# Self-attention's last two units and the context factors of batch 1: packed reciprocals, a GpSimd block, three borrowed tiles

## The chip, the cores and the metric

The kernel runs on one core of a Trainium2 chip. Its time is the device time of one execution in microseconds (us). The core has a matrix engine (TensorE, "PE" in the profile, its weight loads "PEld"), a vector engine (VectorE, "DVE"), an activation engine (ScalarE, "ACT"), a general engine (GpSimd, "POOL") and a sync engine (SyncE, "SP") that here issues nearly all DMAs. Each engine runs its instructions in order; semaphores tie them together.

## The reference, cut to what matters

```
x = x + xcond(layernorm(x), cond, ctx)      # x: 2 x 1024 tokens x 256, fp32
x = x + ffn(layernorm(x))

xcond(x):  h = adaln(x);  x = x + softmax(q k^T / 8) v @ wo + bo   # self-attention, 16 heads of 64
           h = adaln(x);  x = x + cross-attention(h, ctx) @ wo + bo # 16 heads, 77 context rows
           h = adaln(x);  x = x + (a * gelu(gate)) @ w2 + b2        # a, gate = split(h @ w1 + b1)
ffn(x):    two "bit-linear" layers (activations rounded to 8 bits, weights to -1, 0, 1), gelu between
```

## The kernel before, in words

**Self-attention** is cut into 32 units u = 0 to 31 (batch, pair of heads, half of the queries), each with 8 blocks kb of 128 keys. A tile of a block is 128 keys x 1024 (two heads x 512 queries). The order of the work of PE, DVE, ACT and POOL is written by hand in a loop over slots, two blocks to a slot and four slots (q = 0 to 3) to a unit; SP's DMAs are placed by the tile framework's scheduler. In slot s:

- PE makes the scores of two blocks into one of two double PSUM banks (pool ps2, tag "s"), ACT copies them out to sT (L941), DVE takes the running maximum macc (L363).
- After a unit's last block, the maximum over keys is folded: DVE transposes (max_turned, L368), reduces (max_folded, L372 to L385), SP writes the row of 1024 maxima to DRAM (md, L386) and reads it back broadcast to 128 partitions (wide, L387). Two slots later max_placed copies wide into PSUM (mb, ACT L391).
- DVE subtracts mb from a block (shifted, L400); block 5 (POOL_KB) is subtracted on POOL instead (L395), except in unit 31. ACT takes exp (L404), POOL adds the blocks up in pacc (L411), PE multiplies by v (times_v, L419), seven slots after the scores.
- The row sums: PE multiplies pacc by ones. For units 0 to 29 the sums come out packed in four quarters (L451), go through DRAM to a small tile "few" (sums_packed), DVE inverts 128 x 8 numbers (inverted_packed, L482), and they come back broadcast as rinv. For units 30 and 31 the sums come out broadcast (sums_by_ones, L440; unit 31 sums sT itself block by block into tot_last), and DVE inverts 4 x 128 columns in place (inverted, L492). POOL multiplies the unit's output aT by rinv (normalised, L495).

**Cross-attention** has been turned into two small factors per batch, G (scores = h1T x G, 128 x 2464 numbers) and U (output = p x U), kept in DRAM as gd and ud. Its 16 blocks of 128 tokens, each in two halves of 8 heads, run as: cross_scores (PE, L748, bank "s"), cross_shifted (DVE maximum L763 and subtraction L766), cross_exp (ACT L775), cross_divided (DVE L780, L781; POOL L782), cross_turned (PE transposes pt_a and pt_b, L794; ACT and DVE copies pT, L802 to L805), cross_out (PE L815), cross_added (DVE L827). Blocks 0 to 2 of it (the dictionary "tail") start while the last two units of self-attention finish (slots 128 to 133); po_last (L281) is self-attention's last output product. Blocks 3 to 15 run in a second hand-written loop, whose step n makes scores for block n and output for block n - 1.

G and U live in a pool "gu" with two buffers. The G of batch 1 therefore takes the buffer of batch 0's G when block 7 has made its scores (load_g(1), L722), and the U of batch 1 that of batch 0's U (load_u(1), L728 to L732).

**The ternary weights** of the last layers are made in the same loop: DVE and POOL scale, clip and round raw into wq (bf16), PE transposes them (ternary_turned, pt_w, L1116, in the PSUM bank with tag "f"), ACT copies the result to w1T and w2T (L1118, L1120).

**The feed-forward stage** (pu L1582, po L1608) and the bit-linear layers follow in an order that a small planner writes with assumed costs. It is a second hand-ordered stretch, and the framework's scheduler may set instructions of it among the last of the first.

Of the kernel before, what the change touches and what calls it, by code (L numbers as in the profile page):

```python
# [43 lines left out]
def block_kernel(ctx: ExitStack, tc: tile.TileContext, a: dict, out: bass.AP):  # L44
# [8 lines left out]
    def two_banks(name):  # L53
        return ps2.tile([P, 1024], FP, tag="s", name=name)
# [131 lines left out]
    with ExitStack() as sa:  # L186
# [202 lines left out]
        def max_placed(u):  # L389
            mbs[u] = psx.tile([P, 1024], FP, tag="mb", name="mb")  # L390
            nc.scalar.copy(mbs[u], wides[u])  # L391

            if u < NU - 1:
                t = sT[u, POOL_KB]
                nc.gpsimd.tensor_tensor(t, t, wides[u], ALU.subtract)  # L395

        def shifted(u, kb):
            if kb == POOL_KB and u < NU - 1:
                return
            nc.vector.tensor_tensor(sT[u, kb], sT[u, kb], mbs[u], ALU.subtract)  # L400

# [57 lines left out]
        def summed(u):  # L459

            if u in paccs:
                tots[u] = two_banks("tot")
                if u < NU - 2:
                    sums_in_quarters(tots[u], paccs.pop(u))
                else:
                    sums_by_ones(tots[u], paccs.pop(u), True, True)
            rinvs[u] = p1.tile([P, 512], FP, tag="rinv", name="rinv")
            n = 256 if u < NU - 2 else 512
            nc.scalar.copy(rinvs[u][:, :n], tots.pop(u)[:, :n])

        def sums_packed(u):
# [243 lines left out]

        Gs, Us = {}, {}

        def load_g(b):
            Gs[b] = gu.tile([P, GU], FP, tag="gu", name="G")[:, : DC * HK].rearrange(
                "p (c k) -> p c k", c=DC  # L720
            )
            nc.sync.dma_start(out=Gs[b], in_=gd[b])  # L722

        def load_u(b):
            Us[b] = gu.tile([P, GU], FP, tag="gu", name="U").rearrange("p (c d) -> p c d", d=D)
# [9 lines left out]


        norms, prs2, scs2 = {}, {}, {}
        HB = 4

        def cross_scores(n, half):  # L740

            b, qb = n // TB, n % TB
            hT = norms[1, b].hT
            sc = two_banks("sc2")
            for i in range(2):
                at = (half * 2 + i) * HB * CTX
                for c in range(DC):
                    nc.tensor.matmul(  # L748
                        sc[:, i * 512 : i * 512 + HB * CTX],
                        lhsT=hT[:, c, qb * P : (qb + 1) * P],  # L750
                        rhs=Gs[b][:, c, at : at + HB * CTX],
                        start=(c == 0),
                        stop=(c == DC - 1),
                    )
            scs2[n, half] = sc
# [17 lines left out]
        def cross_exp(n, half):  # L773
            ph = prs2[n, half][:, :HALF]
            nc.scalar.activation(ph, ph, AF.Exp)  # L775
# [156 lines left out]
        def settle():  # L932
            while due:
                due.pop(0)()

        for slot in range(NS + 12):
            u, q = slot // SLOTS, slot % SLOTS

            new = [(u, 2 * q + i, scores(u, 2 * q + i)) for i in range(2)] if slot < NS else []
            for v, kb, sc in new:  # L940
                nc.scalar.copy(sT[v, kb], sc)  # L941
            v, k = (slot - LAG + 1) // SLOTS, (slot - LAG + 1) % SLOTS
            old = [(v, 2 * k + i) for i in range(2)] if 0 <= v < NU else []
            if q:
                settle()
            for job in inner.pop(slot, []):
                job[0](*job[1:])
            if q == 2 and 0 <= u - 1 < NU:
                max_placed(u - 1)
            for at in tail.get(slot, []):  # L950
                cross_scores(*at)

            fold = q == 0 and 0 <= u - 1 < NU
            if q == 2:
                for at in new:
                    running_max(*at)
            late = q == 2 and slot < NS
            if not late:  # L960
                exponentials(old)
            settle()
            if fold:
                max_turned(u - 1)
            if q != 2:
                for at in new:
                    running_max(*at)
            if fold:
                max_folded(u - 1)
            for at in tail.get(slot, []):  # L970
                cross_shifted(*at)
                cross_exp(*at)
            for at in tail.get(slot - 1, []):
                cross_divided(*at)
            if q == 1 and 0 <= u - 3 < NU - 2:
                inverted_packed(u - 3)
            w, k = (slot - LAG) // SLOTS, (slot - LAG) % SLOTS
            if 0 <= w < NU:
                for i in range(2):
                    if w == NU - 1:  # L980
                        if k + i == 0:
                            tots[w] = piece_bank("tot_last")
                        sums_by_ones(tots[w], sT[w, 2 * k + i], k + i == 0, k == SLOTS - 1 and i == 1)
                    times_v(w, 2 * k + i)
                if k == SLOTS - 1:
                    evacuated(w)
            if slot == NS + 6:
                summed(NU - 1)
                for part in range(4):
                    inverted(NU - 1, part)  # L990
                normalised(NU - 1)
            elif q == 2 and 0 <= u - 3 < NU - 2:
                normalised(u - 3)
            elif slot == NS + 5:
                for part in range(4):
                    inverted(NU - 2, part)
                normalised(NU - 2)
            for job in extras.pop(slot, []):
                job[0](*job[1:])
            if slot in (NS + 7, NS + 8):  # L1000
                n = slot - NS - 7
                cross_turned(n, 0)
                cross_turned(n, 1)
                cross_added(n, cross_out(n))
            if slot in pieces:
                pieces[slot][0](*pieces[slot][1:])
            if q == 0 and 0 <= u - 3 < NU - 1:
                summed(u - 3)
                if u - 3 < NU - 2:
                    sums_packed(u - 3)  # L1010
            if late:
                exponentials(old)
            if slot >= NS:
                settle()
# [68 lines left out]
        def ternary_scale(name):  # L1083
            pm = piece_bank("pm")
            nc.tensor.matmul(
                pm[:, 0:1], lhsT=ones, rhs=parts[name][:, 0:1], start=True, stop=True
            )
            sw = sws[name] = const.tile([P, 1], FP, name="sw_" + name)
            nc.vector.tensor_scalar(sw, pm[:, 0:1], 1.0 / (F * D), 1e-5, ALU.mult, ALU.max)
            inv = parts[name] = small.tile([P, 1], FP, tag="winv", name="winv")  # L1090
            nc.vector.reciprocal(inv, sw)
            wqs8[name] = p1.tile([P, 2048], BF, tag="macc" if name == "w1" else "wide", name="wq")

        def ternary_clip(name, i, low, engine):
            t = raws[name][i]
# [11 lines left out]
        def ternary_turned(name, k):  # L1107

            wq = wqs8[name]
            pt = psx.tile([P, 8, P], BF, tag="f", name="pt_w")  # L1110
            for i in range(8):
                if name == "w1":
                    at = i * D + k * P
                else:
                    at = i % 2 * F + (4 * k + i // 2) * P
                nc.tensor.transpose(pt[:, i, :], wq[:, at : at + P], ident_bf)  # L1116
            if name == "w1":
                nc.scalar.copy(w1T[:, k, :], pt.rearrange("p f q -> p (f q)"))  # L1118
            else:
                nc.scalar.copy(  # L1120
                    w2T[:, 4 * k : 4 * k + 4, :].rearrange("p a d -> p (a d)"),
                    pt.rearrange("p f q -> p (f q)"),
                )

        for k, name in enumerate(("w1", "w2")):
            for i in range(2):
                at_slot(after, 7 + 2 * k + i, ternary_sum, name, i)
                at_slot((mid, after)[i], (15, 16)[k], ternary_turned, name, i)
            at_slot(mid, (10, 12)[k], ternary_scale, name)
        at_slot(after, 10, ternary_clip, "w1", 0, False, nc.gpsimd)  # L1130
        at_slot(after, 11, ternary_clip, "w1", 0, True, nc.gpsimd)
# [6 lines left out]
        for n in range(3, NT + 1):  # L1138
# [6 lines left out]
            if n < NT:  # L1145
                cross_exp(n, 0)
                cross_divided(n, 0)
                cross_scores(n, 1)
                cross_shifted(n, 1)
                if n == TB - 1:  # L1150
                    load_g(1)
            cross_turned(n - 1, 1)
            if n < NT:
                cross_exp(n, 1)
            po = cross_out(n - 1)
            if n - 1 == TB - 1:
                load_u(1)
            if n < NT:
                cross_divided(n, 1)
            cross_added(n - 1, po)  # L1160
# [520 lines left out]
```

## Time and profile before

| | |
|---|---|
| time, median of 3 runs | 1197.65 us (1196.11, 1197.65, 1202.05) |
| the profiled execution | 1200.08 us; span 1198.3 us from its first to its last instruction |
| busy share of the span | PE 97%, DVE 79%, ACT 68%, POOL 68% |
| TensorE clock granted, mean | 0.985 |
| DMA | 63.24 MB, mean 53 GB/s |

The page gives busy time by engine, the span in 40 slices, the DMA queues, the chain of work that ended last, and the costliest groups. The timeline gives instructions in order of start: start us, duration us, engine, line, operation, output<-inputs, sizes, count; in brackets the idle time of the engine before it and what ended that. SPq lines are DMA issues, not transfers. A PE line's duration is modelled and overlaps the next one's start a little. A fp32 matrix product shows as two records, a transpose as one.

### The profile page before, as it was taken

Reading aid. Unit: us, or ns where it says so; the run is one execution under the profiler, and the core shown is the slowest. Engines: PE = TensorE matmul, PEld = TensorE weight load, DVE = VectorE, ACT = ScalarE, POOL = GpSimd, SP = SyncE. Lnnn points to the kernel's source line nnn. Section 1 sums busy time; section 2 is a strip of 40 time slices with the busy share of each in tenths; the row PEclk is TensorE's granted clock in tenths of the full one; section 3 lists DMA queues with packets and bytes.
Section 4 is the critical chain, followed back from the end, with each engine's and each line's share of the span. In section 5 each row is a group of like instructions: output and inputs, shape, how many; then the busy total and the mean of one; then the engine's idle time right before and its main releaser. Section 6 shows DMA issues by size and latency. Waiting matters only on the chain.

```text
span 1198.3 us, 16887 instructions
## 1 busy us (share of the span) xinstructions
PE 1160.1 (97%) x6005; PEld 573.0 (48%) x6005; DVE 945.3 (79%) x1398; ACT 808.9 (68%) x1032; POOL 810.6 (68%) x625
## 2 busy tenths in 40 slices
PE   8898999999999999999999999999999999999996
PEld 4342334334334343343433332346878866486684
DVE  4779889879888987998888989984767753578596
ACT  4688888888887887888789788651343431555366
POOL 5579888888888888889888999941425315433244
PEclk8999999999999999999999999999999999999996
DMA  7101222212122211311213112211020021000000
GB/s 230 36 27 32 79 64 64 69 47 74 45 79 60 64 58 54 88 41 47 65 53 125 37 46 89 83 60 36 1 76 10 1 62 36 1 18 10 9 10 27
DMA packets 66013, 63.24 MB, mean 53 GB/s; under 512 B 22935, under 2 KB 56329, under 8 KB 65417
## 3 DMA queue, kind: packets, MB, share of 16 engines
q1 hardware_dynamic: 65865, 62.15, 17.2%
q8 instruction: 47, 0.77, 0.3%
q14 instruction: 37, 0.30, 0.1%
q10 hardware_dynamic: 64, 0.02, 0.0%
HBM read 54.63 MB, written 7.52 MB: 52 GB/s over the span
## 4 chain that ended last, share of the span: by engine, by line
PE 79%; DVE 13%; ACT 5%; issue 2%; DMA 1%; POOL 1%; DVEq 0%; SPq 0%; ACTq 0%; POOLq 0%
PE sc L347 16%; PE pav L419 15%; PE pp L281 9%; PE pu L1582 9%; PE sc L748 5%; PE po L815 5%; PE pv L281 4%; DVE macc L363 4%; PE po L1608 4%; DVE sT L400 4%; PE po L281 2%; ACT sT L941 2%; PE pu L1437 1%; PE tot L451 1%; PE po L1484 1%
## 5 line engine op out<-in xcount | busy, mean ns | idle before, releaser
L411 POOL TENSOR_TENSOR pacc<-pacc,sT 128x1024 f32<-128x1024 f32 x186 | 441.2, 2372 | 50.6 <-ACT sT L404 40.7
L941 ACT COPY sT<-sc 128x1024 f32<-128x1024 f32 x256 | 248.0, 1016 | 57.0 <-PE sc L347 49.3
L363 DVE TENSOR_TENSOR macc<-macc,sc 128x1024 f32<-128x1024 f32 x192 | 233.7, 1217 | 65.5 <-ACT sT L941 53.8
L404 ACT ACTIVATE sT<-sT 128x1024 f32<-128x1024 f32 x256 | 260.0, 1062 | 15.9 <-DVE sT L400 14.6
L347 PE MATMUL sc<-qT,kT 64*128 64x512 f32 x1024 | 258.8, 620 | 7.9 <-DVE macc L363 6.7
L400 DVE TENSOR_TENSOR sT<-sT,mb 128x1024 f32<-128x1024 f32 x225 | 261.8, 1206 | 3.1 <-ACT mb L391 3.1
L419 PE MATMUL pav<-sT,v 128*64 128x512 f32 x1024 | 250.2, 606 | 3.0 <-ACT sT L404 2.7
L347 PEld LDWEIGHTS sc<-qT,kT 64*128 64x128 f32 x1024 | 85.6, 185 | 148.5 <-DVE macc L363 66.3
L419 PEld LDWEIGHTS pav<-sT,v 128*64 128x64 f32 x1024 | 62.4, 136 | 151.9 <-issue 76.0
L1582 PE MATMUL pu<-h2T,ffw 128*128 128x512 f32 (+1 forms) x320 | 114.6, 509 | 0.0
L782 POOL TENSOR_TENSOR pr<-pr,t 128x616 f32<-128x616 f32 x32 | 39.2, 1226 | 104.2 <-DVE t L781 57.6
L411 POOL TENSOR_TENSOR pacc<-sT 128x1024 f32<-128x1024 f32 x31 | 73.9, 2383 | 29.8 <-ACT sT L404 29.5
L1582 PEld LDWEIGHTS pu<-h2T,ffw 128*128 128x128 f32 x320 | 59.5, 190 | 44.0 <-issue 39.9
L748 PE MATMUL sc<-G,h1T 128*128 128x308 f32 x256 | 74.1, 433 | 4.9 <-DVE pr L766 3.6
L815 PE MATMUL po<-U,pT 128*128 128x256 f32 (+1 forms) x320 | 74.4, 387 | 3.9 <-ACT pT L805 2.4
L395 POOL TENSOR_TENSOR sT<-sT,wide 128x1024 f32<-128x1024 f32 x31 | 73.8, 2381 | 2.4 <-ACT sT L941 2.4
L815 PEld LDWEIGHTS po<-U,pT 128*128 128x128 f32 (+1 forms) x320 | 60.2, 193 | 13.4 <-ACT pT L805 3.2
L281 PE MATMUL pp<-h1T,wk 128*64 128x512 f32 x256 | 62.3, 608 | 0.9 <-ACT h1T L555 0.9
L281 PE MATMUL pv<-wv,h1T 128*64 128x256 f32 x512 | 60.9, 380 | 1.4 <-ACT qT L299 0.7
L281 PE MATMUL pp<-h1T,wq 128*64 128x512 f32 x256 | 60.5, 593 | 0.0
L748 PEld LDWEIGHTS sc<-G,h1T 128*128 128x128 f32 x256 | 47.6, 194 | 24.1 <-issue 9.6
L1600 DVE SCALAR_TENSOR_TENSOR gT<-pu,vecT,ge 128x512 f32<-128x512 f32 (+1 forms) x40 | 25.6, 641 | 42.0 <-ACT ge L1593 41.7
(185 smaller groups left out, 1520.7 us busy)
## 6 DMA issues: line engine op xcount, KB each, us to landing
wide<-md SPq DMA_DIRECT2D x32, 512.0 KB
rinv<-td SPq DMA_DIRECT2D x60, 128.0 KB
ffw<-in_L_xcond_ff_w_dram SPq DMA_DIRECT2D x3, 1024.0 KB
gd<-cw SPq DMA_DIRECT2D x32, 77.0 KB
ud<-cw SPq DMA_DIRECT2D x32, 77.0 KB
G<-gd SPq DMA_DIRECT2D x2, 1232.0 KB
wk<-in_L_xcond_attn_wk_dram SPq DMA_DIRECT2D x16, 128.0 KB
wq<-in_L_xcond_attn_wq_dram SPq DMA_DIRECT2D x16, 128.0 KB
```

The costliest lines, as they stand in the source:

```text
L281: nc.tensor.matmul(dst[half, :], lhsT=lhsT[:, half], rhs=rhs, start=start, stop=stop)
L347: nc.tensor.matmul(sc[:, j * 512 : (j + 1) * 512], lhsT=kTs[b, pair][rows, kb * P : (kb + 1) * P], rhs=qTs[b, pair][rows, qh * 512 : (qh + ...
L363: nc.vector.tensor_tensor(maccs[u], old, sc, ALU.max)
L395: nc.gpsimd.tensor_tensor(t, t, wides[u], ALU.subtract)
L400: nc.vector.tensor_tensor(sT[u, kb], sT[u, kb], mbs[u], ALU.subtract)
L404: nc.scalar.activation(t, t, AF.Exp)
L411: nc.gpsimd.tensor_tensor(paccs[u], old, t, ALU.add)
L419: nc.tensor.matmul(pavs[u][j * DH : (j + 1) * DH, :], lhsT=vs[b, pair // 2][:, kb, at : at + DH], rhs=sT[u, kb][:, j * 512 : (j + 1) * 512 ...
L748: nc.tensor.matmul(sc[:, i * 512 : i * 512 + HB * CTX], lhsT=hT[:, c, qb * P : (qb + 1) * P], rhs=Gs[b][:, c, at : at + HB * CTX], start=( ...
L815: nc.tensor.matmul(po[:, :D], lhsT=pT2s[n, part][:w, i * P : (i + 1) * P], rhs=Us[b][:w, half * 5 + c, :], start=(half + c == 0), stop=(ha ...
L941: nc.scalar.copy(sT[v, kb], sc)
L1582: nc.tensor.matmul(pu[:, k * 512 : k * 512 + n], lhsT=ffw1[c][:, at : at + P], rhs=hT[:, c, at0 : at0 + n], start=(c == 0), stop=(c == DC ...
```

## The change

- Unit 30 packs its sums as units 0 to 29 do: four quarter products (128 x 256) in place of two (64 x 512), five small DMAs, an inversion of 128 x 8 in place of 4 x 128 x 128, and normalised(30) one slot later, ahead of unit 31's.
- Block 5 of unit 31 is subtracted on POOL, as in all other units.
- Unit 29's sums go into the "f" bank ("tot_f") and no longer into a bank "s".
- In the tail's slots cross_shifted and cross_exp come ahead of max_turned and max_folded.
- G is held as eight pieces of 128 x 308. Batch 1's are in three tiles of self-attention's pool p1: three pieces with tag macc, three with tag wide, two with tag xn, by three DMAs. load_g(1) is called at n = 4, load_u(1) at n = 7 ahead of the transposes. As self-attention's last macc and wide are unit 31's, two of the tiles come free in the tail.
- wq of both ternary weights, which had tags macc and wide, is one tile of "gu"; the last transposes of w2 are called ahead of the last cross_out and use a bank "s".

```diff
@@ -390,12 +390,11 @@
             mbs[u] = psx.tile([P, 1024], FP, tag="mb", name="mb")
             nc.scalar.copy(mbs[u], wides[u])
-            if u < NU - 1:
-                t = sT[u, POOL_KB]
-                nc.gpsimd.tensor_tensor(t, t, wides[u], ALU.subtract)
+            t = sT[u, POOL_KB]
+            nc.gpsimd.tensor_tensor(t, t, wides[u], ALU.subtract)
         def shifted(u, kb):
-            if kb == POOL_KB and u < NU - 1:
+            if kb == POOL_KB:
                 return
             nc.vector.tensor_tensor(sT[u, kb], sT[u, kb], mbs[u], ALU.subtract)
@@ -459,13 +458,11 @@
         def summed(u):
             if u in paccs:
-                tots[u] = two_banks("tot")
-                if u < NU - 2:
-                    sums_in_quarters(tots[u], paccs.pop(u))
-                else:
-                    sums_by_ones(tots[u], paccs.pop(u), True, True)
+                tots[u] = piece_bank("tot_f") if u == NU - 3 else two_banks("tot")
+                sums_in_quarters(tots[u], paccs.pop(u))
             rinvs[u] = p1.tile([P, 512], FP, tag="rinv", name="rinv")
-            n = 256 if u < NU - 2 else 512
+            n = 256 if u < NU - 1 else 512
             nc.scalar.copy(rinvs[u][:, :n], tots.pop(u)[:, :n])
         def sums_packed(u):
@@ -715,11 +712,29 @@
         Gs, Us = {}, {}
+        HB = 4
+        PIECE = HB * CTX
         def load_g(b):
-            Gs[b] = gu.tile([P, GU], FP, tag="gu", name="G")[:, : DC * HK].rearrange(
-                "p (c k) -> p c k", c=DC
-            )
-            nc.sync.dma_start(out=Gs[b], in_=gd[b])
+            if b == 0:
+                t = gu.tile([P, GU], FP, tag="gu", name="G")
+                held = [t[:, : 8 * PIECE]]
+            else:
+                held = [
+                    p1.tile([P, 1024], FP, tag=tag, name="G1")[:, : n * PIECE]
+                    for tag, n in (("macc", 3), ("wide", 3), ("xn", 2))
+                ]
+            at = 0
+            flat = gd[b].rearrange("p c k -> p (c k)")
+            for t in held:
+                n = t.free_size()
+                nc.sync.dma_start(out=t, in_=flat[:, at : at + n])
+                Gs.setdefault(b, []).extend(
+                    t[:, k : k + PIECE] for k in range(0, n, PIECE)
+                )
+                at += n
         def load_u(b):
             Us[b] = gu.tile([P, GU], FP, tag="gu", name="U").rearrange("p (c d) -> p c d", d=D)
@@ -735,7 +750,6 @@
         norms, prs2, scs2 = {}, {}, {}
-        HB = 4
         def cross_scores(n, half):
@@ -743,12 +757,11 @@
             hT = norms[1, b].hT
             sc = two_banks("sc2")
             for i in range(2):
-                at = (half * 2 + i) * HB * CTX
                 for c in range(DC):
                     nc.tensor.matmul(
-                        sc[:, i * 512 : i * 512 + HB * CTX],
+                        sc[:, i * 512 : i * 512 + PIECE],
                         lhsT=hT[:, c, qb * P : (qb + 1) * P],
-                        rhs=Gs[b][:, c, at : at + HB * CTX],
+                        rhs=Gs[b][c * 4 + half * 2 + i],
                         start=(c == 0),
                         stop=(c == DC - 1),
                     )
@@ -960,6 +973,9 @@
             if not late:
                 exponentials(old)
             settle()
+            for at in tail.get(slot, []):
+                cross_shifted(*at)
+                cross_exp(*at)
             if fold:
                 max_turned(u - 1)
             if q != 2:
@@ -967,12 +983,9 @@
                     running_max(*at)
             if fold:
                 max_folded(u - 1)
-            for at in tail.get(slot, []):
-                cross_shifted(*at)
-                cross_exp(*at)
             for at in tail.get(slot - 1, []):
                 cross_divided(*at)
-            if q == 1 and 0 <= u - 3 < NU - 2:
+            if q == 1 and 0 <= u - 3 < NU - 1:
                 inverted_packed(u - 3)
             w, k = (slot - LAG) // SLOTS, (slot - LAG) % SLOTS
             if 0 <= w < NU:
@@ -985,16 +998,13 @@
                 if k == SLOTS - 1:
                     evacuated(w)
             if slot == NS + 6:
+                normalised(NU - 2)
                 summed(NU - 1)
                 for part in range(4):
                     inverted(NU - 1, part)
                 normalised(NU - 1)
             elif q == 2 and 0 <= u - 3 < NU - 2:
                 normalised(u - 3)
-            elif slot == NS + 5:
-                for part in range(4):
-                    inverted(NU - 2, part)
-                normalised(NU - 2)
             for job in extras.pop(slot, []):
                 job[0](*job[1:])
             if slot in (NS + 7, NS + 8):
@@ -1006,8 +1016,7 @@
                 pieces[slot][0](*pieces[slot][1:])
             if q == 0 and 0 <= u - 3 < NU - 1:
                 summed(u - 3)
-                if u - 3 < NU - 2:
-                    sums_packed(u - 3)
+                sums_packed(u - 3)
             if late:
                 exponentials(old)
             if slot >= NS:
@@ -1089,7 +1098,9 @@
             nc.vector.tensor_scalar(sw, pm[:, 0:1], 1.0 / (F * D), 1e-5, ALU.mult, ALU.max)
             inv = parts[name] = small.tile([P, 1], FP, tag="winv", name="winv")
             nc.vector.reciprocal(inv, sw)
-            wqs8[name] = p1.tile([P, 2048], BF, tag="macc" if name == "w1" else "wide", name="wq")
+            if name == "w1":
+                t = gu.tile([P, 2 * GU], BF, tag="gu", name="wq")
+                wqs8["w1"], wqs8["w2"] = t[:, :2048], t[:, 2048:4096]
         def ternary_clip(name, i, low, engine):
             t = raws[name][i]
@@ -1107,7 +1118,8 @@
         def ternary_turned(name, k):
             wq = wqs8[name]
-            pt = psx.tile([P, 8, P], BF, tag="f", name="pt_w")
+            pool, tag = (ps2, "s") if (name, k) == ("w2", 1) else (psx, "f")
+            pt = pool.tile([P, 8, P], BF, tag=tag, name="pt_w")
             for i in range(8):
                 if name == "w1":
                     at = i * D + k * P
@@ -1125,7 +1137,8 @@
         for k, name in enumerate(("w1", "w2")):
             for i in range(2):
                 at_slot(after, 7 + 2 * k + i, ternary_sum, name, i)
-                at_slot((mid, after)[i], (15, 16)[k], ternary_turned, name, i)
+                if (k, i) != (1, 1):
+                    at_slot((mid, after)[i], (15, 16)[k], ternary_turned, name, i)
             at_slot(mid, (10, 12)[k], ternary_scale, name)
         at_slot(after, 10, ternary_clip, "w1", 0, False, nc.gpsimd)
         at_slot(after, 11, ternary_clip, "w1", 0, True, nc.gpsimd)
@@ -1147,14 +1160,16 @@
                 cross_divided(n, 0)
                 cross_scores(n, 1)
                 cross_shifted(n, 1)
+                if n == TB // 2:
+                    load_g(1)
                 if n == TB - 1:
-                    load_g(1)
+                    load_u(1)
             cross_turned(n - 1, 1)
             if n < NT:
                 cross_exp(n, 1)
+            if n == NT:
+                ternary_turned("w2", 1)
             po = cross_out(n - 1)
-            if n - 1 == TB - 1:
-                load_u(1)
             if n < NT:
                 cross_divided(n, 1)
             cross_added(n - 1, po)
```

## The prediction

> **What bounds the kernel now.** I read the page's chain first, then the chain of waits and PE's timeline from 748 to 985 us, then SP's, ACT's and DVE's timelines where PE stood idle.
>
> ```profile
> PE 79%; DVE 13%; ACT 5%; issue 2%; DMA 1%; POOL 1%; DVEq 0%; SPq 0%; ACTq 0%; POOLq 0%
> ```
>
> PE is the bound. Between 755 and 978 us it is idle for over half a microsecond at five places only, so the change can win there and lose where it breaks up PE's work. The largest place is in the tail (timeline):
>
> ```profile
> 780.78 4.00 PE L748 MATMUL sc<-G,h1T 128*128 128x308 f32 x8 [3.57 <-DVE pr L766]
> ...
> 786.54 0.72 ACT L775 ACTIVATE pr<-pr 128x616 f32<-128x616 f32 x1 [2.56 <-DVE pr L766]
> ...
> 787.17 1.01 ACT L391 COPY mb<-wide 128x1024 f32<-128x1024 f32 x1
> ...
> 788.20 2.35 DVE L400 TENSOR_TENSOR sT<-sT,mb 128x1024 f32<-128x1024 f32 x2 [0.75 <-ACT mb L391]
> ...
> 789.46 2.19 ACT L404 ACTIVATE sT<-sT 128x1024 f32<-128x1024 f32 x2 [1.29 <-DVE sT L400]
> ...
> 792.99 1.08 PE L440 MATMUL tot_last<-sT,ones 128*64 128x512 f32 x4
> ```
>
> PE waits 3.57 us for DVE to leave a bank "s": unit 29's sums took the other one, and the subtraction L766 stands behind the whole fold of unit 31. The eight records then take 4.00 us against 2.27 for the next such eight (786.64 in the chain of waits), at half clock (0.50 in the windows). mb of unit 31 stands behind an exp that waits for the same subtraction. Unit 31's first block passes DVE, ACT and PE with some slack: its exp is out by about 790.5, PE comes at 793.
>
> SP's timeline has the way of the maximum, first in an ordinary unit, then in unit 31; the windows tell when the broadcast's traffic ends:
>
> ```profile
> 688.53 0.33 SPq L386 DMA_DIRECT2D md<-mrow  x1
> 689.00 0.52 SPq L473 DMA_DIRECT2D td<-rinv  x1
> 689.91 0.31 SPq L387 DMA_DIRECT2D wide<-md  x1
> ```
> ```profile
> 777.31 0.34 SPq L1064 DMA_DIRECT2D raw<-in_L_ffn_w_dram  x1
> 779.08 0.34 SPq L386 DMA_DIRECT2D md<-mrow  x1
> 781.73 0.52 SPq L473 DMA_DIRECT2D td<-rinv  x1
> 782.35 0.39 SPq L387 DMA_DIRECT2D wide<-md  x1
> ```
> ```profile
> 784.00:786.00 2.00, 2.00 (x9) 0.77 (x9) 1.15 (x2) 0.00 (x0) 1.92 (x2) 0.94 0.50 166
> 786.00:788.00 2.00, 2.00 (x10) 1.08 (x7) 1.42 (x4) 1.46 (x2) 2.00 (x2) 1.00 0.04 8
> ```
>
> Normally wide is issued 1.38 us after md. In unit 31 it takes 3.27, because td of unit 29 is between them and waits for ACT. The traffic is over by about 786.
>
> The last two places, batch 1's G and the end of cross-attention (PE's and ACT's timelines):
>
> ```profile
> 883.60 2.31 PE L748 MATMUL sc<-G,h1T 128*128 128x308 f32 x8 [1.28 <-DMA G<-gd]
> ...
> 968.89 1.94 PE L1582 MATMUL pu<-h2T,ffw 128*128 128x512 f32 x4
> 969.09 1.01 ACT L1118 COPY w1T<-pt_w 128x1024 bf16<-128x1024 bf16 x1 [2.02 <-PE pt_w L1116]
> ```
>
> **The change, part by part.** All by line numbers of before.
>
> A, the tail. In the built order the second cross_scores waits for nothing, so PE loses neither the 3.57 us nor the 4.00 - 2.27 = 1.73 us of half clock: PE's own work would reach tot_last at 793.06 - 5.30 = 787.8. What is late next is unit 31's maximum. DVE now makes the cross maximum and subtraction (L763, L766: from 779.05 to 780.64, 1.59 us) before the fold, so mrow ends at 779.05 + 1.6 = 780.6, not 779.05. On SP td of unit 29 is now ahead of md: unit 29's sums are ready at 777.2 and ACT's exp of the first half at 777.7, so td leaves near 778.1, before md is due. A piece of G (462 KB) is also ahead of md, and few of unit 29 ahead of wide. I take 1.4 us from md to wide and 0.5 for the traffic of G: wide at 782.5, 0.15 later than now, landing near 786.1. ACT's exp before mb is then out (DVE: two blocks to 782.9, 1.6 more, exp 0.72: 785.2). So mb 786.1 to 787.1, first subtraction 1.2, exp 1.06: 789.4. PE waits 789.4 - 787.8 = 1.6 us there and is at tot_last 3.7 us earlier than 793.06. From there PE has 5.7 us of work in each slot, DVE 4.8 (788.20 to 793.02 per slot): PE leads. Unit 30's sums in quarters take 0.57 against 0.86: 0.3. A = 4.0. Ends: 5.6 if the maximum is in time for PE, 0.2 if it is 2.1 later still (462 of the 1232 KB that took 5.66 us in the chain, all in md's way) and the wait then halves the clock for one window (1.7).
>
> Two parts cost nothing. POOL's subtraction of block 5 (2.38 us, mean of L395) starts when pacc of unit 30 is done near 788 and one L782 after it; ACT wants the block two slots after mb, near 799. DVE loses 1.2 us there and is not the bound. Unit 30's packing adds five DMAs and takes 3.39 us from DVE at 808.30, where DVE has been ahead of PE. The trip from td to the inversion took 5.1 us in the ordinary unit (689.00 to 694.07, with waits); from PE's new sums near 799.0, behind 512 KB of raw, it ends by 806.5. DVE's inversion of few stands before the last cross total and unit 31's inversion, which needs ACT near 809: cover 2.5 us, and what exceeds it would go to PE one for one. normalised(30) then ends near 811, and po_last wants it at 822. On SP the second ffw (812.68) and U queue behind it and are wanted at 969 and 899.
>
> B, batch 1's G. Its last piece is read from DRAM near 792, so block 8 finds it there. PE's 1.28 us go, and nothing near it is late next: the transposes after it wait for POOL's L782, which ends at 883.15, 1.7 us before they would start. U is issued earlier too. B = 1.3; ends 0 and 1.4. The matmuls read pieces of the same 308 columns: no cost.
>
> C, the end of cross-attention. Today the scheduler puts six records of pu (1.77 + 0.86 = 2.63 us in the chain) between the transposes pt_w, where PE would otherwise wait for ACT. In the built order of the new kernel no pu comes before the last output product, and pt_w of w2 follows pt_w of w1 at once, in the same bank. So PE waits until ACT's copy ends at 970.10, then pt_w 0.45, pt_a 0.87; ACT's copy of w2T (1.01) ends at 971.8; then pt_b 0.22, pt_w 0.45, po 4.33: 976.8, and pu starts from nothing. Today it starts again at 977.84 with 2.63 done, as if at 975.2. C = -1.6. From 978.0 to 1006.38 PE makes 66 records in 28.38 us, 0.43 each, without a gap, so this reaches the end. Ends: 0 if later stages take it up, -3.3 if the break also halves the clock for a window.
>
> On that clock: in this trace PE gaps of 1.22 and 1.28 us (748.02, 882.32) kept 1.00, while 1.78 us at 962.28 was followed by 0.50 from 965.1 to 968.5, and the 12 records of po at 964.06 took 4.48 against 2.86. My new waits of 1.6 and 1.1 us lie between; I take no half clock. The Trainium skill ("TensorE: Matmul & The Clock Gate", Why this matters for your kernels) advises against idle gaps over about 3 us; the trace already pays at 1.78. By the page neither new wait would cost anything, as in my sum. Its section "What's actually happening" calls the window free-running, which would let the same gap cost 1.7 us in one run and nothing in the next.
>
> Sum: -4.0 - 1.3 + 1.6 = -3.7 us. On the profiled execution 1200.08 gives 1196.4; the median is 2.43 lower, so 1197.65 - 3.7 = 1194.0.
>
> **The rivals.**
>
> R1, slower: unit 31's maximum becomes PE's pace. Place: SP's queue, with G's piece ahead of md and few ahead of wide. Each microsecond beyond my 782.5 goes to PE, and 1.7 more once its wait halves the clock; the gain is gone from 2.0 us on. Price: 1.9 (the delay that one small DMA between md and wide causes today) plus 1.6 (the rest of G's 2.1) is 3.5: -3.7 + 3.5 + 1.7 = +1.5, 1199.2 us. For it: raw's transfer at 777.31 is still busy when G's is issued. The Trainium skill ("DMA: Bandwidth & Descriptors", HWDGE ordering) says that each DMA engine consumes a ring's descriptors in order, which speaks against putting G first; md behind raw's 512 KB landed before 782.35 all the same. Against: G leaves near 778.7, md two microseconds later.
>
> R2, faster: A reaches its good end (5.6 + 0.3), C is taken up later: -5.9 - 1.3 = -7.2, 1190.4 us. For it: the last 100 us are a chain of short steps that leave PE waiting. Against: PE's unbroken run after 978.
>
> R3, the stall at G doesn't go but moves to another wait at block 8: B = 0, -2.4, 1195.3 us. Against: U's transfer is over before 900 even today.
>
> **How the numbers follow.** Forecast 0.52 (1192.2 to 1196), R1 0.15, R2 0.21, R3 0.12. Half a percent, 6.0 us, is about what a measurement here can tell from no change: faster is below 1191.7, slower above 1203.6. R2 and a little of the forecast are faster: 0.25. Nothing that I have priced reaches 1203.6; I leave 0.07 for what I have not seen. Same 0.68. The range is 1189.5 to 1199.5, from R2 to R1.
>
> **What would show it.** Right: no wait of PE for L766 near 777 and no half clock there; a wait of 1 to 2 us at the first tot_last, behind exp; tot_last some 4 us earlier against the same start; the first product of block 8 without a DMA wait; no pu before the last po, and PE idle about 1.1 us between the two pt_w. Wrong: wide more than 2 us after md in unit 31, PE at half clock after tot_last's wait, DVE waiting for few, or pu starting no later than now relative to block 15.

## The result, and the profile after

| | before | after |
|---|---|---|
| time, median of 22 runs each | 1197.76 us (1196.11 to 1202.29) | 1201.95 us (1198.96 to 1205.21) |
| ratio to before, 95% interval | | 1.0031 (1.0022 to 1.0039) |
| profiled execution, span | 1198.3 us | 1199.0 us |
| granted clock, mean | 0.985 | 0.987 |

The change costs 3.7 us by the ratio (0.0031 x 1198; the two medians differ by 4.2), where 3.7 us less had been forecast. "Half clock" stands for a granted clock of 0.50. The two profiled spans differ by only 0.7 us, for two reasons of the clock. The profile of after reaches the first cross score 1.48 us earlier (770.95 against 772.43), 1.2 us of it by 60 us, as the half clock at the program's start lasted 3.4 us in it and 6.8 us in the other. And behind a gap of 1.78 us at 962 us the profile of before lost 1.6 us to half clock, that of after nothing behind the same gap. All readings of the tail below are therefore relative to that first cross score. Line numbers are those of the kernel that a view belongs to.

The page's chain of waits can't be set beside the one of before: in after it is followed back over 18% of the span only.

The timeline of PE in the tail of after shows where the time went (start, duration, engine, line, operation, output and inputs; in brackets the idle time before it and what ended that):

```profile
775.66 2.34 PE L761 MATMUL sc<-G,h1T 128*128 128x308 f32 x8
...
788.46 1.67 PE L439 MATMUL tot_last<-sT,ones 128*64 128x512 f32 x4 [2.18 <-ACT sT L403]
791.34 1.97 PE L418 MATMUL pav<-sT,v 128*64 128x512 f32 x4 [1.21 <-ACT aT L435]
793.10 1.92 PE L439 MATMUL tot_last<-sT,ones 128*64 128x512 f32 x4
794.80 1.45 PE L418 MATMUL pav<-sT,v 128*64 128x512 f32 x4
...
815.04 0.43 PE L807 MATMUL pt_b<-ident,pr 128*104 128x128 f32 x2 [2.06 <-ACT rinv L466]
815.53 6.27 PE L828 MATMUL po<-U,pT 128*128 128x256 f32 x20
```

The wait for L766 at 777 is gone, as forecast: sc at 775.66 has no bracket. In its place PE has three waits, and only the first was in the prediction. The four groups of four records of tot_last or pav take 1.45 to 1.97 us each there against 1.03 to 1.08 in before, and 20 products of po take 6.27 us against 4.59 later. The windows of after give the granted clock from 788 to 794 us (last columns: clock, DMA share, GB/s): it falls to 0.70, 0.50 and 0.50.

```profile
788.00:790.00 2.00, 1.54 (x4) 0.20 (x4) 1.90 (x4) 1.47 (x2) 1.81 (x1) 0.70 0.33 121
790.00:792.00 2.00, 0.79 (x4) 0.30 (x4) 1.97 (x4) 1.19 (x2) 0.83 (x1) 0.50 0.55 135
792.00:794.00 2.00, 2.00 (x8) 0.51 (x6) 1.92 (x3) 1.81 (x2) 1.62 (x2) 0.50 0.25 102
```

Who holds the three up is told by the timelines of ACT, POOL and SP in after, in this order:

```profile
785.05 1.02 ACT L391 COPY mb<-wide 128x1024 f32<-128x1024 f32 x1 [1.27 <-DMA wide<-md]
787.35 2.19 ACT L403 ACTIVATE sT<-sT 128x1024 f32<-128x1024 f32 x2 [1.29 <-DVE sT L399]
790.09 0.72 ACT L788 ACTIVATE pr<-pr 128x616 f32<-128x616 f32 x1 [0.56 <-DVE pr L779]
790.72 0.57 ACT L435 COPY aT<-pav 128x512 f32<-128x512 f32 x1
...
814.41 0.59 ACT L466 COPY rinv<-tot_last 128x512 f32<-128x512 f32 x1 [1.81 <-POOL aT L492]
```
```profile
813.11 1.26 POOL L492 TENSOR_TENSOR aT<-aT,rinv 128x512 f32<-128x512 f32 x1 [2.70 <-DMA rinv<-td]
```
```profile
777.28 0.39 SPq L733 DMA_DIRECT2D G<-gd  x1
779.22 0.33 SPq L386 DMA_DIRECT2D md<-mrow  x1
779.64 0.38 SPq L475 DMA_DIRECT2D few<-td  x1
781.71 0.32 SPq L387 DMA_DIRECT2D wide<-md  x1
...
803.26 0.52 SPq L470 DMA_DIRECT2D td<-rinv  x1
...
809.61 1.12 SPq L482 DMA_DIRECT2D rinv<-td  x2
```

- **First tot_last, 2.18 us.** It needs exp of unit 31, which needs mb, which needs the broadcast wide. G's piece leaves at 777.28, ahead of md; wide follows md by 2.49 us and not by 1.4.
- **pav, 1.21 us.** There is one bank "av". Unit 31's first product may not enter it until ACT has copied unit 30's output (aT, L435). PE finished that output at 784; the copy stands on ACT behind mb, two exp of unit 31 and the exp of cross-attention, and runs at 790.72.
- **pt_b, 2.06 us.** Tag "rinv" has one buffer. ACT's copy of unit 31's sums (L466) may not write it until POOL has used unit 30's reciprocals (L492), and these come through five DMAs: td at 803.26, rinv issued at 809.61, POOL at 813.11. pt_b wants bank "f", which tot_last holds until that copy.

The other two places went as forecast. Block 8's first score has no DMA wait any more (PE's timeline of after), and the second pt_w waits for ACT:

```profile
883.75 2.24 PE L761 MATMUL sc<-G,h1T 128*128 128x308 f32 x8
...
968.54 0.61 PE L1128 MATMUL pt_w<-ident_bf,wq 128*128 128x128 bf16 x8 [1.10 <-ACT w1T L1130]
...
975.46 10.04 PE L1597 MATMUL pu<-h2T,ffw 128*128 128x512 f32 x23
```

### The profile page after: what moved, and what is told of

Its sections match the earlier page's. It is cut to its first block, busy times and chain, and to the rows that moved or that the text cites. A ratio compares the mean times of both kernels' runs of the same rounds, so it can differ in the third digit from the quotient of the medians.

```text
span 1199.0 us, 16893 instructions
## 1 busy us (share of the span) xinstructions
PE 1159.5 (97%) x6001; PEld 572.0 (48%) x6009; DVE 941.8 (79%) x1394; ACT 808.7 (67%) x1032; POOL 813.3 (68%) x626
## 3 DMA queue, kind: packets, MB, share of 16 engines
q1 hardware_dynamic: 66609, 62.43, 16.9%
## 5 line engine op out<-in xcount | busy, mean ns | idle before, releaser
L394 POOL TENSOR_TENSOR sT<-sT,wide 128x1024 f32<-128x1024 f32 x32 | 76.2, 2380 | 2.2 <-DMA wide<-md 2.2
L1623 PE MATMUL po<-ffw,gT 128*128 128x256 f32 x256 | 57.3, 379 | 0.0
```

The costliest lines, as they stand in the source:

```text
L1623: nc.tensor.matmul(po[:, :D], lhsT=self.gT[:, f, k * P : (k + 1) * P], rhs=ffw2[:, f, :], start=(f == 0), stop=(f == FS - 1),)
```

## The experiments

Two theories. **Q**: the loss is in queues and single buffers that the prediction didn't list, pav behind ACT and pt_b behind the packing. **M**: it is unit 31's maximum, late behind G's piece (rival R1), and the later waits follow from that.

All times are ratios to the kernel before on the same chip. From each profile PE's timeline gives three stretches of the tail: **I** from the first cross score to the first tot_last, **II** on to pt_a of block 0, **III** on to the first score of block 3.

| kernel | ratio (95%) | I | II | III | sum |
|---|---|---|---|---|---|
| before | | 20.56 | 19.58 | 20.77 | 60.91 |
| after | 1.0031 (1.0022, 1.0039) | 17.51 | 23.43 | 23.04 | 63.98 |
| own buffer for unit 31's sums | 1.0021 (1.0009, 1.0032) | 17.99 | 23.47 | 20.82 | 62.28 |
| unit 30 not packed | 1.0010 (0.9999, 1.0021) | 18.01 | 23.38 | 20.77 | 62.16 |
| unit 30's output copied first | 1.0001 (0.9989, 1.0012) | 17.89 | 19.34 | 22.85 | 60.08 |
| G behind the maximum | 1.0007 (0.9996, 1.0018) | 16.98 | 21.31 | 23.14 | 61.43 |
| all three mended | 0.9959 (0.9943, 0.9974) | 16.57 | 19.35 | 20.82 | 56.74 |
| the same, w2 back, pT first | 0.9943 (0.9926, 0.9960) | 16.74 | 19.35 | 19.60 | 55.69 |
| before with G's tiles alone | 0.9993 (0.9978, 1.0007) | 21.75 | 19.58 | 20.77 | 62.10 |
| before with the order alone | 0.9980 (0.9968, 0.9992) | 16.44 | 23.31 | 20.77 | 60.52 |
| w2 back | 1.0013 (1.0003, 1.0024) | 18.11 | 23.06 | 23.18 | 64.35 |
| block 5 back on DVE | 1.0026 (1.0015, 1.0037) | 17.70 | 23.29 | 23.16 | 64.15 |
| buffer and copy, G ahead | 0.9969 (0.9954, 0.9983) | 17.76 | 19.34 | 20.82 | 57.92 |
| best version, unpacked | 0.9945 (0.9931, 0.9959) | 16.60 | 19.59 | 19.77 | 55.96 |

**Own buffer for unit 31's sums** (on after):

```diff
-            rinvs[u] = p1.tile([P, 512], FP, tag="rinv", name="rinv")
+            pool, tag = (p1, "rinv") if u < NU - 1 else (p2, "wo")
+            rinvs[u] = pool.tile([P, 512], FP, tag=tag, name="rinv")
```

> The changed kernel, but unit 31's sums get a buffer of their own instead of waiting for the one that unit 30's packed reciprocals still hold. Theory Q (the new queues): ACT's copy of unit 31's sums stood behind POOL's last use of unit 30's reciprocals, so behind the five small DMAs. Then the wait of 2.06 us at pt_b goes, and with it the half clock that followed (6.27 us for 20 records of po against 4.59 later); some 1.0 us comes back where DVE copies pT behind its own inversion, as before the change. About 2.7 us less than the changed kernel: 1.0008 of the kernel before. Theory M (unit 31's maximum, rival R1): the tail is late by what happens before 796; PE then only waits at the next place for DVE's inversion, under 1 us is won: 1.002 to 1.003 of before.

Stretch III falls from 23.04 to 20.82, the value of before, and the wait at pt_b from 2.06 to 0.15 us (PE's timeline of this run):

```profile
817.49 0.43 PE L808 MATMUL pt_b<-ident,pr 128*104 128x128 f32 x2 [0.15 <-ACT rinv L467]
...
821.46 2.43 PE L829 MATMUL po<-U,pT 128*128 128x256 f32 x10 [0.96 <-DVE pT L817]
```

The single buffer is what PE waits for, and 0.96 us comes back at po, as expected. The price is 2.2 us in the profile and 1.2 us in the ratios, whose intervals overlap; 2.7 was too much. By the ratio alone 1.0021 would be theory M's number, and theory Q's 1.0008 lies just outside the interval; for Q speaks that the wait is gone and only 0.96 us of it comes back. Two more pairs of ratios that differ in this wait give 2.5 us (the next experiment against after) and 3.8 us (0.9969 against 1.0001, both with the copy first).

**Unit 30 not packed** (on after): sums over 512 columns and DVE's inversion as before.

```diff
+                if u < NU - 2:
                     sums_in_quarters(tots[u], paccs.pop(u))
+                else:
+                    sums_by_ones(tots[u], paccs.pop(u), True, True)
...
-                sums_packed(u - 3)
+                if u - 3 < NU - 2:
+                    sums_packed(u - 3)
+            elif slot == NS + 5:
+                for part in range(4):
+                    inverted(NU - 2, part)
+                normalised(NU - 2)
```

> The changed kernel without the packing of unit 30's reciprocals: its sums are made over 512 columns and inverted by DVE in four parts (3.39 us) as in the kernel before; all else stays. Theory Q: the same gain as from the buffer, 2.7 us, less 0.3 for the longer sums: 1.001 of before. Theory M: DVE's 3.39 us more cost PE nothing and nothing is won: 1.003 of before.

Stretch III is 20.77 again, and the ratio is theory Q's. Both ways of taking the round trip off unit 31's path give the same stretch to 0.05 us, so it is the trip behind a single buffer, not DVE's load, that costs.

**Unit 30's output copied first** (on after): its last two products and the copy aT are called ahead of the exponentials of the slot; only ACT's order changes.

```diff
+            if slot == NS + 2:
+                for i in range(2):
+                    times_v(NU - 2, TB - 2 + i)
+                evacuated(NU - 2)
...
-            if 0 <= w < NU:
+            if 0 <= w < NU and slot != NS + 2:
```

> The changed kernel, but ACT's copy of unit 30's output (aT from pav) stands right behind its copy mb, ahead of the two exp of unit 31 and the exp of the second cross-attention block. Theory Q: PE's wait of 1.21 us for the only bank av goes, and the half clock from 792.2 to 795.6 probably with it (about 1.4): 1.2 to 2.6 us less than the changed kernel, 1.001 to 1.002 of before. Theory M: PE waits for unit 31's exp instead, the same time: 1.003 of before.

It won 3.6 us, more than theory Q's 2.6. ACT makes the copy in idle time and PE goes from tot_last to pav without a wait (ACT's and PE's timelines of this run):

```profile
787.53 1.02 ACT L391 COPY mb<-wide 128x1024 f32<-128x1024 f32 x1 [1.64 <-DMA wide<-md]
788.49 0.58 ACT L435 COPY aT<-pav 128x512 f32<-128x512 f32 x1
```
```profile
790.95 1.08 PE L439 MATMUL tot_last<-sT,ones 128*64 128x512 f32 x4 [2.56 <-ACT sT L403]
791.86 1.03 PE L418 MATMUL pav<-sT,v 128*64 128x512 f32 x4
```

Stretch II falls from 23.43 to 19.34: 1.21 us of wait and 2.9 us more, all but 0.2 of it half clock, are gone, although the wait at tot_last is 2.56 us here. That no half clock follows it can be this profile's luck (see the last section); the wait at pav is gone whatever the clock does. Theory M, by which PE would only wait for exp instead (1.003, outside the interval), falls for this wait.

**G behind the maximum** (on after): a small write on POOL holds the tile of G's first piece.

```diff
             nc.gpsimd.tensor_tensor(t, t, wides[u], ALU.subtract)
+            if u == NU - 1:
+                late = p1.tile([P, 1024], FP, tag="macc", name="late")
+                nc.gpsimd.memset(late[:, :8], 0.0)
```

> The changed kernel, but the first piece of batch 1's G (462 KB) leaves behind the broadcast of unit 31's maximum instead of ahead of it (a write of eight columns on GpSimd holds its tile until then). Theory M: the broadcast leaves 1.1 us sooner and lands 1.5 to 2 us sooner; PE's wait of 2.18 us at the first tot_last falls to about 0.7 and no half clock follows (2.8 us in the two windows to 795.6): 3 to 4 us less, 1.000 to 1.001 of before. Theory Q: the broadcast is not held by G but by few's DMA and by the length of the fold; it lands within 0.5 us of now, the wait at pav stays, under 1 us is won: 1.002 to 1.003 of before.

The ratio is theory M's, and theory Q's 1.002 lies outside the interval, but the way is neither's. Wide now follows md by 1.42 us (785.27 and 783.85), and tot_last waits 1.65 us, not 0.7. The wait at pav, for a copy that stands behind the exp, doesn't go but grows to 1.80 (PE's timeline of this run):

```profile
795.43 1.08 PE L421 MATMUL pav<-sT,v 128*64 128x512 f32 x4 [1.80 <-ACT aT L438]
```

Of the 2.9 us in the ratio the profile has 0.5 in stretch I and 2.1 in II; the 2.1 are the half clock that this profile doesn't have, less 0.6 for the longer wait at pav. So M has a true part: the piece does delay the maximum.

**All three mended** (the buffer, the copy and G's piece):

> The changed kernel with three edits together: a buffer of its own for unit 31's sums, unit 30's output copied ahead of unit 31's exp, batch 1's G behind the maximum. If the three waits were the whole of what the prediction missed, the tail (first cross score to the first score of block 3, 60.9 us before and 64.0 after) falls to 57 to 57.5: the 60.1 of the run with the output copied first, less 0.9 for the maximum, less 2.2 for pt_b and up to 1.3 for its half clock, plus 1.0 for the copy of pT. Then the whole stands at what was predicted, 0.997 of before. If the waits only pass the time on to one another, the tail stays at 60 and the time at 1.000 of before.

0.9959, 4.9 us below the kernel before and 8.6 below after. One wait is left in stretches I and II, the one that the prediction had (PE's timeline of this run):

```profile
788.06 1.08 PE L442 MATMUL tot_last<-sT,ones 128*64 128x512 f32 x4 [1.25 <-ACT sT L406]
788.97 1.03 PE L421 MATMUL pav<-sT,v 128*64 128x512 f32 x4
```

Its SP timeline shows the maximum without G ahead, wide 1.43 us after md:

```profile
779.76 0.34 SPq L386 DMA_DIRECT2D md<-mrow  x1
780.35 0.33 SPq L479 DMA_DIRECT2D few<-td  x1
781.19 0.32 SPq L387 DMA_DIRECT2D wide<-md  x1
```

**The same, with w2 back and pT first** (the three edits, step C undone, and DVE's copy of pT ahead of its inversion of unit 31's sums):

```diff
-            if n == NT:
-                ternary_turned("w2", 1)
...
-                if (k, i) != (1, 1):
-                    at_slot((mid, after)[i], (15, 16)[k], ternary_turned, name, i)
+                at_slot((mid, after)[i], (15, 16)[k], ternary_turned, name, i)
...
-                for part in range(4):
-                    inverted(NU - 1, part)
-                normalised(NU - 1)
...
                 cross_turned(n, 1)
+                if n == 0:
+                    for part in range(4):
+                        inverted(NU - 1, part)
+                    normalised(NU - 1)
```

> The same three edits, and two more: the transposes of w2's second half stand behind the last output product again, in the bank they had before the change, so that six products of the next stage can fill PE's wait (step C undone); and DVE copies pT ahead of its inversion of unit 31's sums. Expected: 1.6 us less from the first (step C), 1.0 less from the second: 0.995 of before, tail 56 to 56.5. If step C was only paid for in this one profile, 0.996 to 0.997.

Stretch III loses the 0.96 us at po and 0.25 more (20.82 to 19.60). This is the best version with 0.9943; the step from 0.9959 lies within the intervals, so its parts rest on the profiles.

**Before with G's tiles alone**: load_g, cross_scores, wq's tile and the call of load_u from after, all else from before.

> The kernel before with one part of the change alone: batch 1's G in three tiles that self-attention has left, loaded early, U behind it, and the ternary weights in the place of G. Step B: PE's wait of 1.28 us at block 8 goes, the tail stays at 60.9 since the copy mb is held by an exp until 787 in that order: 1.3 us less, 0.999 of before. If G's piece ahead of the maximum costs time in any order (theory M), mb moves past 787.2 by about 1 us and nothing is won: 1.000.

0.9993; the interval holds both the 1.3 us and none. In the profile block 3 to block 8 takes 48.81 us (836.12 to 884.93) against 50.26 before: the DMA wait is gone. Stretch I is 1.2 us longer, all of it in a half clock after the old wait of 3.58 us that lasted two windows of 3.4 us and not one; there is no wait at tot_last in it, so the piece ahead of the maximum is covered in the old order.

**Before with the order alone**:

```diff
-                tots[u] = two_banks("tot")
+                tots[u] = piece_bank("tot_f") if u == NU - 3 else two_banks("tot")
...
             settle()
+            for at in tail.get(slot, []):
+                cross_shifted(*at)
+                cross_exp(*at)
             if fold:
                 max_turned(u - 1)
...
-            for at in tail.get(slot, []):
-                cross_shifted(*at)
-                cross_exp(*at)
```

> The kernel before with another part alone: the sums of unit 29 in bank f, and the cross maximum and subtraction ahead of the fold of unit 31; no packing of unit 30, no block of unit 31 on GpSimd, G as before. Theory Q: the 3.57 us and the half clock there go (5.3), a wait of 1.5 to 2 us at the first tot_last and one of 1.2 to 1.8 at pav come, with half clock in some runs: 0.6 to 2.5 us less, 0.998 to 0.9995 of before, tail 58.5 to 60.3. Theory M: with no G in front of the maximum PE waits about 1 us at tot_last and not at pav, 4 us less: 0.9965, tail 57.

Theory Q's number (2.4 us less); theory M's 0.9965 lies just outside the interval. The wait at pav is 1.80 us in it, with neither G nor packing in the kernel: it belongs to the new order itself. tot_last waits 1.12 us (PE's timeline of this run):

```profile
788.28 1.08 PE L440 MATMUL tot_last<-sT,ones 128*64 128x512 f32 x4 [1.12 <-ACT sT L404]
791.16 1.88 PE L419 MATMUL pav<-sT,v 128*64 128x512 f32 x4 [1.80 <-ACT aT L436]
```

**w2 back** (step C undone in after, by the first two hunks of the best version's diff and the old bank).

> The changed kernel with step C alone undone: w2's last transposes stand behind the last output product again, in bank f. Expected from step C: PE's idle 1.1 us between the two pt_w is filled with products of the next stage, 1.6 us less than the changed kernel, 1.0018 of before (the changed kernel was at 1.0031). If step C costs nothing on average (the kernel before lost 1.6 us to a half clock at this place in the profiled run, the changed one did not): 1.003.

2.2 us less than after; the intervals just overlap. At the same full clock, from the last 12 products of po in block 14 to the first pu after block 15 it takes 965.78 to 977.88, 12.10 us with 2.63 us of pu already made, thus 9.47; after takes 964.13 to 975.46, 11.33. Step C costs 1.86 us.

**Block 5 back on DVE** (on after):

```diff
+            if u < NU - 1:
                 t = sT[u, POOL_KB]
                 nc.gpsimd.tensor_tensor(t, t, wides[u], ALU.subtract)
...
-            if kb == POOL_KB:
+            if kb == POOL_KB and u < NU - 1:
```

> The changed kernel with block 5 of unit 31 back on DVE. The prediction gave this part no price: DVE has 1.7 us of idle time in that slot, PE leads, 1.003 of before. If the subtraction on GpSimd (2.36 us) holds something up (the normalisation of unit 29 behind it, or the tile of the maximum, which G's second piece waits for), or if it relieves DVE where DVE counts, the time moves by about 1 us: 1.002 or 1.004.

1.0026, and the three stretches are those of after to 0.2 us: this part moves nothing that can be measured.

**Buffer and copy, G ahead**:

> The changed kernel with two of the three edits: the buffer for unit 31's sums and the earlier copy of unit 30's output; batch 1's G stays ahead of unit 31's maximum. Against the run with all three (0.9959, tail 56.7 us, 1.25 us of wait at the first tot_last) this prices G's piece alone: a wait of 2.2 to 2.7 us at the first tot_last, 0.9 to 1.4 more, and a half clock behind it in some runs (1.7): tail 57.7 to 59.8, 0.997 to 0.998. If G's piece costs nothing once the other two are mended: 0.996.

0.9969 against 0.9959: 1.2 us for G's piece, which the intervals alone would not show, and 1.19 in stretch I (17.76 to 16.57), the rest being equal to 0.01. Over all profiles the wait at tot_last is 2.18 to 2.79 us with the piece ahead in the new order (seven kernels) and 1.12 to 1.65 without (five). Whether the piece holds the maximum up by its place in the queue or by its traffic, no run tells.

**Best version, unpacked**:

> The best version so far (three edits, w2 back, pT ahead of the inversion: 0.9943, tail 55.7 us) with the packing of unit 30's reciprocals left out, so its sums are 512 wide and DVE inverts them itself; the buffer of its own is then not needed. If packing is worth what the prediction gave it, 0.3 us of PE's time and nothing else: 0.9945. If it spares DVE time that counts here: 0.996 or more; if its five small DMAs cost something even with the buffer: below 0.994.

0.9945. In the profile the packing is worth 0.24 us in stretch II and 0.17 in III: next to nothing, and it was what had made the third wait.

## Why the prediction was wrong

The forecast for the three stretches was 20.56 - 3.7 = 16.9, 19.58 - 0.3 = 19.3 and 20.77. The kernel with the three edits measures 16.57, 19.35 and 20.82. So the sum of step A came true to 0.3 us for a kernel without three things that the changed kernel has. In stretch I that is partly luck: the forecast held 0.5 us for G's traffic, and that kernel has no G ahead of the maximum; with it there, stretch I takes 17.76. Of the prediction's own signs of being wrong three came: wide 2.49 us after md, half clock behind tot_last's wait, and DVE waiting for few (0.34 us).

1. **"Two parts cost nothing", the packing (step A).** This failed. The prediction asked who wants unit 30's output (po_last at 822, and it was in time) and whether DVE would wait for few. It didn't ask who wants the buffer. POOL's use of the reciprocals was to end near 811; it begins at 813.11, as they land only then, and ends at 814.37. ACT's copy of unit 31's sums, which the prediction had not tied to it, has to wait until 814.41. 2.2 us in stretch III, priced at 0.
2. **"From there PE leads" (step A).** This failed too. The prediction laid PE's work in a slot (5.7) against DVE's (4.8) and followed ACT's queue only to unit 31's first exp. In before the copy aT ended at 793.40, half a microsecond ahead of the pav at 793.89 that needs its bank (ACT's and PE's timelines of before); moving PE earlier used that cover up. 1.21 us of wait in after, priced at 0. The experiment with the order alone shows this wait (1.80 us) without any other part of the change.

```profile
792.83 0.57 ACT L436 COPY aT<-pav 128x512 f32<-128x512 f32 x1
...
793.89 1.03 PE L419 MATMUL pav<-sT,v 128*64 128x512 f32 x4
```

3. **"PE waits 789.4 - 787.8 = 1.6 us there" (step A).** A term that was mis-sized by 0.6 in this profile and 0.9 on average: without G the wait is 1.12 to 1.65, so the 0.5 us given to G's traffic and the 1.4 from md to wide were too little for a piece of 462 KB ahead. Rival R1 had this mechanism at the right place and priced it too high: 2.1 us for G in all (0.5 in the sum and 1.6 more) where it is 1.2, and 1.9 for few between md and wide, which no run shows: few stands there in the kernel with the three edits too, and wide follows md by 1.43.
4. **"I take no half clock".** In after the waits brought 2.9 us more to stretch II, the value of 1.7 having been kept for the range only. All but 0.2 of it is clock: with a wait of 1.80 at pav and no half clock, stretch II is 21.31 = 19.34 + 1.80 + 0.17 (G behind the maximum). It is not the one profile alone: all five kernels with the new order, G ahead and the copy not first have two windows of half clock there and a stretch II of 23.06 to 23.47. For a wait of the size foreseen the term held: behind 1.25 to 1.65 us at tot_last no half clock came (four profiles).
5. **B, -1.3.** Right: block 3 to block 8 is 1.44 us shorter in after (50.26 to 48.82), 1.45 in the experiment.
6. **C, +1.6.** Right: 1.86 us at equal clock.
7. **Block 5 on GpSimd, 0.** Right.

The range ended at 1199.5 with R1, since every bad case was built on the one chain that the prediction had followed. With 2.2 and 1.2 us for the two missed waits and 2.9 for the clock the sum is -3.7 + 0.6 + 1.2 + 2.9 + 2.2 + 0.3 = +3.5, the 0.3 being step C's excess; 3.7 was measured. These terms are read from one profile, so that they meet the ratio this closely is partly chance.

The Trainium skill ("DMA: Bandwidth & Descriptors", HWDGE ordering: the descriptors of a ring are consumed in order on each DMA engine) spoke against G ahead of md, and the 1.2 us agree with it. Its advice on idle gaps ("TensorE: Matmul & The Clock Gate", Why this matters for your kernels: none over about 3 us) would have let all three waits of after pass; the profile has half clock after 2.18 and 2.06 us.

## What to carry to other kernels

When work is moved earlier, list for each instruction of it not only the data but the buffer it writes, and who empties that buffer from where in which queue: a copy that was in time by 0.5 us behind three long instructions is late once its reader comes 4 us sooner. A round trip that is cheap for the engine it relieves holds its single buffer for the whole trip. Where two waits may fall within a few microseconds, price them together.

## What the runs showed of the hardware

In all 14 profiles the half clock comes in pieces of 3.41 us (some in a row) whose starts, within one execution, differ by multiples of 3.41. Where a gap falls on that grid decided its price: the same gap of 1.77 to 1.78 us before the last 12 products of po in block 14 was followed by half clock in the five profiles where it began 0.44 to 0.79 us after a point of the grid, and not in the nine where it began 1.2 to 3.4 us after one. The Trainium skill ("TensorE: Matmul & The Clock Gate", What's actually happening) names a free-running window of 3413 ns, which these profiles agree with: the first piece begins 7.7 to 11.0 us after the span's start, spread over the whole step. At tot_last waits of 2.18 to 2.79 us that began 0.3 to 1.1 us after a point brought half clock (five profiles), and two of 2.44 and 2.56 us that began 2.5 us after one did not. The part of the grid that counts is not the same at every place: an earlier gap of 1.80 to 1.82 us before scores near 737 us was followed by half clock in eight profiles where it began 0.27 to 0.49 us after a point and in one where it began 0.12 us ahead of one, and not in five where it began 0.67 us, or 2.8 to 3.0 us, after one. Why is open.
